# Layer 1's sums regrouped between the steps and a closing part ordered by single operations

## The chip, the cores and the metric

The kernel runs on one core of a Trainium2 chip. A core has five engines with instruction queues of their own: TensorE (PE, matrix products into the accumulators called PSUM), VectorE (DVE), ScalarE (ACT), GpSimd (POOL) and SyncE (SP, which here only issues transfers). [...] The metric is the device time of one launch in microseconds (us), the median of several runs.

## The reference

Two graph layers follow each other over N = 4096 nodes with D = 64 features and one 4096 x 4096 adjacency matrix of zeros and ones.

```python
# layer 0: the last 100 neighbours of a row, weighted by powers of 1/2
rank = cumsum(adj != 0, axis=1); deg = rank[:, -1:]; k = minimum(deg, 100)
w = mask * where(rank - (deg - k) > 0, 0.5 ** (k - (rank - (deg - k))), 0)
x1 = layernorm(x + w @ (x @ W0) + b0)
# layer 1: the mean over the neighbours and the row itself, a dense layer, L2 normalisation
h = (adj @ x1 + x1) / (deg + 1)
z = relu(concat([x1, h]) @ W1 + b1)
out = layernorm(x1 + z / maximum(norm(z), 1e-12))
```

## The kernel before

**Tiles.** The transposed adjacency is cut into 8 slabs `g` of 512 output rows and 8 columns `k` of 512 inputs. A tile `A[g][k]` (128 partitions x 4 x 512, bf16, 512 KB in SBUF) is loaded once by a transfer that POOL issues (`load_next`, line 98), and used twice: for layer 0's weights when it comes in, and for layer 1's sum when all x1 of column `k` is there. The pool `a16` has 33 such buffers; a load waits until one is free.

**The 64 steps** (lines 539 to 576) run over the slabs 0 to 7, each with its columns from 7 to 0. A step has four parts on PE: `weigh` (line 270, 32 small products into two PSUM tiles `v`), some counting (`count`, `spread`), one block of layer 1 (`some_sums`, line 339: four products of 128x512 that add column `k` into slab `g`), and `gather` (line 300, four products of 128x512) for the weights of the step before. The weights `w` are made from `v` by ACT (line 294, the first half) and DVE (line 295, the second half); the next `weigh` writes into the same two PSUM tiles and so waits for both.

**Which blocks** go with the steps is in `jobs` (lines 317 to 321), one list entry for a run of columns of one slab. A run sums in one PSUM bank; at its end `evict_part` (line 331) moves the bank into SBUF: the first time for a slab by a copy on ACT (line 337), later by an addition to `part[g]` on DVE (line 334). The DVE instruction stands in the queue behind the step's `w` and ahead of what is hooked to the step (`run(i, DVE)`). A block may run from step `8(k+1)+7` on. There is one block a step, except in the steps of `SAVED`. Before the change 39 of 64 blocks run with the steps; 25 are left.

**Hooks of layer 0.** For slab `g`, with i = 8(g+1): the projection `first_pz` in step i+1, its moments in i+2, the root (lines 364 to 368) in i+3, x1 itself (line 441, four instructions on DVE) in i+4, its high half (line 446, ACT) and low half in i+5 and i+6, transposes and the dense part c1 until i+8.

**The closing part** (line 759 on) is an order written out by hand: what an engine gets in which order is the order of these calls. It holds layer 0's end for slab 7, the 17 blocks left of slabs 0 to 6 (`own`), slab 7 in two halves of 256 rows (`own_half`, 2 x 8 blocks) and then, for a unit of one or two slabs, a chain: the sum's copy or addition into `hT` (line 627 on DVE, or ACT for slab 7, line 632), `last_pz` (line 659, PE), z (664, DVE), relu and square (668, 673, ACT), the row sums ss (680, 681, DVE), the root (378, POOL, by a power), y (698, DVE), the addition of x1 (703; POOL for a unit of a slab or more, DVE for a half slab), mean and variance (387, 389, DVE), a root on POOL, the output o (748, ACT) and the store (SP). Slabs 3 and 7 share a last root on ACT and DVE, and DVE makes half of their outputs (750). PSUM's eight banks are handed round by the list `banks`; two of its tiles, `va` and `vb`, hold two banks each (lines 582 and 583).

Of the kernel before, what the change touches and what calls it, by code (L numbers as in the profile page):

```python
# [40 lines left out]
def adj_resnorm_kernel(  # L41
# [279 lines left out]
    jobs += [(6, [4, 3, 2, 1, 0, 5]), (4, [4, 5]), (0, [4, 5]), (1, [4, 5]), (2, [4])]  # L321
# [303 lines left out]
    def last_hT(g):  # L625
        ep["hT", g] = hT_of(g)
        nc.vector.tensor_tensor(ep["hT", g], acc[g], part[g], ALU.add)  # L627
        banks.append(acc[g])
# [7 lines left out]
    def unit(*slabs):  # L636
        name, bs = "_".join(map(str, slabs)), [g * TB + t for g in slabs for t in range(TB)]
        n = len(bs)
        tiles = []
        for i in range(n // TB):  # L640
            tiles.append(a16p.tile([P, 4 * TB // n, n, D], F32, tag="a16", name=f"u_{name}_{i}"))
        four = [t[:, i] for t in tiles for i in range(4 * TB // n)]
        return name, bs, four

    def half_unit(h):
        _, bs, four = u7
        ts_ = slice(2 * h, 2 * h + 2)
        return f"{L}{'ab'[h]}", bs[ts_], [f[:, ts_] for f in four]

    def rows(bs):  # L650
        return slice(bs[0], bs[-1] + 1)

    def last_pz(u):

        name, bs, _ = u
        pz = ep["pz1", name] = psum(len(bs), D, f"pz1_{name}")
        for t, b in enumerate(bs):
            h = ep["hT", b // TB]
            nc.tensor.matmul(pz[:, t, :], lhsT=h[:, ts(b % TB, P)], rhs=wn_sb, start=True, stop=True)  # L659

    def last_z(u):

        name, bs, (z, _, _, _) = u
        nc.vector.tensor_tensor(z, ep["pz1", name], c1[:, rows(bs), :], ALU.add)  # L664
        free(f"pz1_{name}")

    def last_relu(u):
        nc.scalar.activation(u[2][1], u[2][0], AF.Relu)  # L668

    def last_sq(u):  # L670
        name, bs, (z, sq, _, _) = u
        if len(bs) >= TB:
            nc.scalar.activation(sq, sq, AF.Square)
        else:
            nc.vector.scalar_tensor_tensor(sq, z, 0.0, z, ALU.max, ALU.mult)

    def last_ss(u):
        name, bs, (_, sq, _, _) = u
        ss = ep["ss", name] = small.tile([P, len(bs)], F32, tag="ss", name=f"ss_{name}")
        nc.vector.tensor_reduce(ss, sq, AX.X, ALU.add)  # L680
        nc.vector.tensor_tensor(ss, ss, least[:, rows(bs)], ALU.max)  # L681

    def last_sn(u):
        name = u[0]
        ep["sn", name] = root_a(ep["ss", name], zero, f"n_{name}")

    def last_rn(u):
        name = u[0]
        ss = ep["ss", name]
        if ("sn", name) in ep:  # L690
            ep["rn", name] = root_b(ep["sn", name], ss, zero, f"n_{name}")
        else:
            ep["rn", name] = root_p(ss, None, name, "rn")

    def last_y(u):
        name, bs, (z, _, y, _) = u
        rn = ep["rn", name].unsqueeze(2).to_broadcast([P, len(bs), D])
        nc.vector.scalar_tensor_tensor(y, z, 0.0, rn, ALU.max, ALU.mult)

    def last_add(u):  # L700
        name, bs, (_, _, y, _) = u
        engine = nc.gpsimd if len(bs) >= TB else nc.vector
        engine.tensor_tensor(y, y, x1[:, rows(bs), :], ALU.add)

    mv_37 = small.tile([P, 2 * TB, 2], F32, tag="mv_37", name="mv_37")
    slot_of = {3: 0, L: TB}

    def last_mv(u):
        name, bs, (_, _, y, _) = u
        if bs[0] // TB in slot_of:  # L710
            ep["mv1", "37"] = mv_37
            t = slot_of[bs[0] // TB] + bs[0] % TB
            moments(y, f"l1_{name}", mv_37[:, t : t + len(bs), :])
        else:
            ep["mv1", name] = moments(y, f"l1_{name}")

    def last_s(u):
        name = u[0]
        ep["s1", name] = root_a(ep["mv1", name][:, :, 1], eps_ln, f"l1_{name}")

    def last_r(u):
        name = u[0]
        v = ep["mv1", name][:, :, 1]
        if ("s1", name) in ep:
            ep["r1", name] = root_b(ep["s1", name], v, eps_ln, f"l1_{name}")
        else:
            ep["r1", name] = root_p(v, LN_EPS, name, "r1")

    def offset(u):
        name, bs, _ = u  # L730
        mv, r = ep["mv1", name], ep["r1", name]
        off = ep["off", name] = small.tile([P, len(bs)], F32, tag="off", name=f"off_{name}")
        if ("s1", name) in ep:
            nc.vector.scalar_tensor_tensor(off, mv[:, :, 0], -1.0, r, ALU.mult, ALU.mult)
        else:
            nc.gpsimd.tensor_tensor(off, mv[:, :, 0], r, ALU.mult)
            nc.gpsimd.tensor_scalar(off, off, -1.0, None, ALU.mult)

    def last_o(u, t0, t1, engine=nc.scalar):
        name, bs, (_, _, y, o) = u  # L740
        if bs[0] // TB in slot_of:
            n0 = slot_of[bs[0] // TB]
            mv, r, off = [ep[what, "37"][:, n0 : n0 + TB] for what in ("mv1", "r1", "off")]
        else:
            mv, r, off = ep["mv1", name], ep["r1", name], ep["off", name]
        for t in range(t0, t1):
            if engine is nc.scalar:
                engine.activation(o[:, t, :], y[:, t, :], AF.Identity, bias=off[:, t : t + 1], scale=r[:, t : t + 1])
            else:
                engine.tensor_scalar(  # L750
                    o[:, t, :], y[:, t, :], mv[:, t, 0:1], r[:, t : t + 1], ALU.subtract, ALU.mult
                )

    def store(u):
        name, bs, (_, _, _, o) = u
        for i, b in enumerate(range(0, len(bs), TB)):
            nc.sync.dma_start(out=out[bs[b] // TB], in_=o[:, b : b + TB, :])

    run(NS, DVE)
    gather(*held)  # L760
    own(5, 5)
    first_hT(L)
    banks.append(ps_a.tile([P, R], F32, tag="acc0", name="va0"))
    first_pz(L)
    own(5, 6)
    first_y(L)
    first_mv(L)
    own(4, 6)
    free(f"pz0_{L}")
    first_s(L)  # L770
    own(0, 6)
    first_least(L)
    first_r(L)
    own(1, 6)
    first_x1(L)
    own(2, 5)
    first_hi(L)
    own_half(1, 0)
    first_xl(L)
    own(6, 6)  # L780
    first_lo(L)
    own(6, 7)
    own(4, 7)
    last_hT(6)
    u6 = unit(6)
    last_pz(u6)
    last_hT(4)
    own(5, 7)
    last_z(u6)
    last_relu(u6)  # L790
    own(1, 7)
    last_hT(5)
    last_sq(u6)
    last_ss(u6)
    own(0, 7)
    last_hT(1)
    last_rn(u6)
    u45 = unit(4, 5)
    last_pz(u45)
    last_hT(0)  # L800
    last_y(u6)
    last_add(u6)
    u01 = unit(0, 1)
    last_pz(u01)
    last_z(u45)
    last_mv(u6)
    last_relu(u45)
    last_sq(u45)
    last_r(u6)
    own(2, 7)  # L810
    last_z(u01)
    last_ss(u45)
    own(2, 6)
    last_relu(u01)
    offset(u6)
    last_sq(u01)
    first_px(L)
    last_rn(u45)
    own(3, 7)
    last_hT(2)  # L820
    first_x1T(L)
    free(f"px_{L}")
    last_ss(u01)
    u2 = unit(2)
    last_pz(u2)
    last_o(u6, 2, 4)
    last_o(u6, 0, 2)
    last_y(u45)
    last_rn(u01)
    first_pu(L)  # L830
    last_z(u2)
    store(u6)
    own(3, 6)
    last_relu(u2)
    first_c1(L)
    free(f"pu_{L}")
    last_sq(u2)
    last_add(u45)
    own_half(1, 6)
    last_y(u01)  # L840
    own_half(1, 7)
    last_ss(u2)
    own(3, 5)
    last_add(u01)
    last_mv(u45)
    own_half(1, 1)
    own_half(1, 4)
    last_rn(u2)
    own_half(1, 3)
    own_half(1, 2)  # L850
    last_hT(3)
    own_half(1, 5)
    last_r(u45)
    last_y(u2)
    u3 = unit(3)
    last_pz(u3)
    last_mv(u01)
    half_hT(1)
    u7 = unit(L)
    u7b = half_unit(1)  # L860
    last_pz(u7b)
    own_half(0, 1)
    last_add(u2)
    last_z(u3)
    own_half(0, 7)
    last_z(u7b)
    last_relu(u3)
    own_half(0, 6)
    last_sq(u7b)
    offset(u45)  # L870
    last_ss(u7b)
    own_half(0, 2)
    last_sq(u3)
    last_r(u01)
    own_half(0, 0)
    last_o(u45, 4, 6)
    last_ss(u3)
    own_half(0, 3)
    last_mv(u2)
    last_sn(u7b)  # L880
    own_half(0, 5)
    last_o(u45, 6, 8)
    own_half(0, 4)
    last_rn(u7b)
    last_o(u45, 2, 4)
    last_rn(u3)
    last_y(u7b)
    half_hT(0)
    last_add(u7b)
    last_o(u45, 0, 2)  # L890
    u7a = half_unit(0)
# [74 lines left out]
```

## Time and profile before

| what | value |
|---|---|
| median of 3 runs | 239.58 us (239.44 to 240.66) |
| the profiled execution's own time | 239.75 us |
| its span, first to last instruction | 238.0 us |
| mean granted PE clock | 0.971 of full speed |
| PE busy | 211.8 us, 89% |
| DVE busy | 180.1 us, 76% |
| ACT busy | 136.2 us, 57% |
| POOL busy | 83.3 us, 35% |
| adjacency transfers | 64, 512 KB each in SBUF |

Busy times are of the whole span. The chain of work that ended last is followed back from the last instruction to what released it. A start-to-start distance of two neighbouring instructions of one engine is what an instruction costs in a full queue; its duration in the trace is a little longer[...].

### The profile page before, as it was taken

The page shows a single profiled execution, that of the slowest core. Times are in us where ns is not written, and L with a number is a line of the kernel's source. Part 1 is how long each engine was busy: PE and PEld are TensorE (multiplying, and loading weights), DVE is VectorE, ACT ScalarE, POOL GpSimd, SP SyncE. Part 2 cuts the span into 40 slices and gives each one's busy share as a digit, 9 for nine tenths or more (in the row PEclk, how much of TensorE's full clock was granted, in tenths as well). Part 3 has the DMA queues.
Part 4 walks back from the last instruction along what each step waited for, and adds up shares of the span by engine and source line. Part 5 has one row for each costly group of instructions (what it writes and reads, how often), then busy time and mean ns, then how long its engine had stood idle before and what let it go on. Part 6 is the DMA issues. An engine that isn't in the chain of part 4 may idle for free.

```text
span 238.0 us, 7425 instructions
## 1 busy us (share of the span) xinstructions
PE 211.8 (89%) x3128; PEld 98.4 (41%) x3171; DVE 180.1 (76%) x457; ACT 136.2 (57%) x205; POOL 83.3 (35%) x160
## 2 busy tenths in 40 slices
PE   8689979889997999999999999999999999996920
PEld 2223324234433533443345344434453354765810
DVE  5459788987896699778847975686768765789973
ACT  6058876788676756653655456555645521171582
POOL 8344573432432311213221152214610000277940
PEclk9799999999999999999999999999999999999795
DMA  6999999999999999999999999999930000000021
GB/s 200 209 216 220 212 213 212 222 215 213 220 213 215 214 222 213 212 213 218 218 208 186 193 206 185 187 178 183 196 77 3 3 0 0 3 1 23 3 88 66
DMA packets 11985, 37.34 MB, mean 157 GB/s; under 512 B 1328, under 2 KB 3504, under 8 KB 11952
## 3 DMA queue, kind: packets, MB, share of 16 engines
q0 software_dynamic: 9216, 33.56, 72.4%
q1 hardware_dynamic: 2736, 3.31, 4.5%
q8 instruction: 25, 0.41, 0.6%
q14 instruction: 8, 0.07, 0.1%
HBM read 69.37 MB, written 1.05 MB: 296 GB/s over the span
## 4 chain that ended last, share of the span: by engine, by line
PE 47%; DMA 34%; issue 7%; DVE 7%; POOL 2%; ACT 2%; ACTq 0%; POOLq 0%
DMA a<-in_adjT_dram 34%; PE acc L305 11%; PE acc_part L314 10%; PE v L278 5%; PE cnt L248 4%; PE v L287 3%; PE va L659 2%; PE va L314 2%; PE vb L608 2%; PE pi L528 2%; PE rep L266 1%; PE vb L314 1%; PE ma L314 1%; PE pz L414 1%; ACT w L294 1%
## 5 line engine op out<-in xcount | busy, mean ns | idle before, releaser
L294 ACT ACTIVATE w<-v,less 128x1024 int16<-128x1024 f32 x64 | 71.3, 1113 | 50.4 <-PE v L287 38.0
L295 DVE TENSOR_SCALAR w<-v 128x1024 int16<-128x1024 f32 x64 | 78.2, 1222 | 19.1 <-PE v L287 17.7
L105 POOL DMA_DIRECT2D a<-in_adjT_dram x64 | 35.8, 560 | 97.0 <-PE rep L266 34.4
L305 PE MATMUL acc<-w,xhl 128*128 128x512 bf16 x240 | 66.1, 379 | 2.1 <-issue 1.1
L314 PE MATMUL acc_part<-a,x1hl 128*128 128x512 bf16 x132 | 37.3, 381 | 2.1 <-issue 1.4
L305 PEld LDWEIGHTS <-xhl 128*128 128x128 f16 x256 | 23.1, 98 | 32.7 <-issue 9.1
L268 ACT ACTIVATE near<-rep,most 128x512 bf16<-128x512 f32 x39 | 26.6, 682 | 8.2 <-PE rep L266 8.1
L314 PEld LDWEIGHTS <-x1hl 128*128 128x128 f16 x224 | 18.6, 98 | 30.4 <-issue 14.4
L278 PE MATMUL v<-a,tri 32*32 32x512 bf16 x1024 | 28.7, 385 | 0.5 <-ACT w L294 0.5
L287 PE MATMUL v<-near,mine 32*32 32x512 bf16 x1024 | 27.7, 376 | 0.0
L248 PE MATMUL cnt<-a,pick 128*32 128x512 bf16 x256 | 21.2, 386 | 6.5 <-DMA a<-in_adjT_dram 4.9
L258 DVE TENSOR_TENSOR cs<-cnt,cs 128x512 bf16<-128x512 f32 x31 | 21.2, 685 | 6.4 <-PE cnt L248 6.3
L278 PEld LDWEIGHTS <-tri 32*32 32x32 bf16 x1024 | 9.7, 88 | 19.7 <-issue 19.3
L378 POOL TENSOR_TENSOR rn<-ss,power 128x4 f32<-128x4 f32 (+1 forms) x5 | 6.3, 1276 | 29.0 <-DVE ss L681 28.9
L266 PE MATMUL rep<-cs,further 128*128 128x512 bf16 x39 | 15.0, 385 | 1.0 <-DVE cs L258 1.0
L248 PEld LDWEIGHTS <-pick 128*32 128x32 bf16 x256 | 6.0, 94 | 21.5 <-issue 12.6
L233 POOL TENSOR_TENSOR a<-a,ident_b 128x128 bf16<-128x128 bf16 x32 | 12.7, 429 | 0.1
L287 PEld LDWEIGHTS <-mine 32*32 32x32 bf16 x1024 | 10.3, 87 | 2.5 <-issue 2.4
L659 PE MATMUL va<-wts,hT 128*128 128x64 f32 x64 | 8.8, 292 | 2.4 <-DVE hT L627 1.9
L260 DVE CAST cs<-cnt 128x512 bf16<-128x512 f32 x8 | 5.5, 691 | 6.7 <-PE cnt L248 6.7
L659 PEld LDWEIGHTS va<-wts,hT 128*128 128x128 f32 x64 | 8.4, 206 | 3.7 <-DVE hT L627 2.8
L668 ACT ACTIVATE u<-u 128x256 f32<-128x256 f32 (+1 forms) x5 | 2.5, 502 | 12.4 <-DVE u L664 12.4
(136 smaller groups left out, 241.5 us busy)
## 6 DMA issues: line engine op xcount, KB each, us to landing
a<-in_adjT_dram POOLq DMA_DIRECT2D x64, 512.0 KB, 16.5
c<-in_x_quads_dram SPq DMA_DIRECT2D x2, 512.0 KB, 4.5
x<-in_x_dram SPq DMA_DIRECT2D x8, 128.0 KB, 7.3
out_dram<-u SPq DMA_DIRECT2D x8, 128.0 KB, 1.7
wts<-in_weights_dram SPq DMA_DIRECT2D x1, 160.0 KB, 7.2
```

Of the source, the lines that this page charges most:

```text
L105: nc.gpsimd.dma_start(out=a, in_=adjT[g, k])
L248: nc.tensor.matmul(cnt[g][quarters[q], :], lhsT=pick[:, PW - 4 * k : PW - 4 * k + Q], rhs=A[g][k][:, q, :], start=first, stop=last,)
L258: nc.vector.tensor_tensor(new, cnt[g], cs[g], ALU.add)
L266: nc.tensor.matmul(pr, lhsT=further, rhs=cs[g], start=True, stop=True)
L268: nc.scalar.activation(near[g], pr, AF.Relu, bias=most, scale=-1.0)
L278: nc.tensor.matmul(v[e // 2][quarters[q], e % 2, :], lhsT=tri[quarters[e], :], rhs=A[g][k][quarters[e], q, :], start=True, stop=False,)
L287: nc.tensor.matmul(v[e // 2][quarters[q], e % 2, :], lhsT=mine[quarters[e], 4 * k + q, :], rhs=nr[quarters[e], :], start=False, stop=True,)
L294: nc.scalar.activation(w[:, 0:2, :], v[0], AF.Relu, bias=less)
L295: nc.vector.tensor_scalar(w[:, 2:4, :], v[1], -STEP * MAX_NEIGH, 0.0, ALU.add, ALU.max)
L305: nc.tensor.matmul(acc0[g], lhsT=xhl[:, b, :], rhs=w[:, q, :].bitcast(BF16), start=(k, q) == (NK - 1, 0), stop=(k, q) == (0, KB - 1),)
L314: nc.tensor.matmul(acc, lhsT=x1hl[:, b, :], rhs=A[g][b // KB][:, b % KB, :], start=first, stop=last)
L659: nc.tensor.matmul(pz[:, t, :], lhsT=h[:, ts(b % TB, P)], rhs=wn_sb, start=True, stop=True)
```

## The change

First, `jobs` gets another fifth line. Slab 6 is left wholly to the closing part, as are columns 6 and 7 of every slab; 36 blocks run with the steps and 28 are left. In steps 51 to 60 other blocks run than before, most of them a run of their own; steps 61 to 63 get none.

Second, the closing part is written anew. Every operation has a name in `work`, and one string gives the order of all of them, so that the instructions of one phase (the eight of a mean and variance, the four of a root) can stand apart with others between them. Small results lie in one tile `scratch`. The arithmetic of a unit is as it was, with these differences: x1 is added on DVE for every unit (`DVE_ADDS`), the sum of slab 6 is copied to `hT` by ACT (`COPIED`, it has no `part`), the offset on POOL is the negated mean times the root, and in the last group DVE makes five outputs and ACT three (before four and four).

```diff
-    jobs += [(6, [4, 3, 2, 1, 0, 5]), (4, [4, 5]), (0, [4, 5]), (1, [4, 5]), (2, [4])]
+    jobs += [(0, [4]), (1, [4]), (2, [4]), (4, [4, 5]), (5, [5]), (3, [5]), (0, [5]), (1, [5]), (2, [5])]
...
-    def last_hT(g):
+    def slab_hT(g):
         ep["hT", g] = hT_of(g)
-        nc.vector.tensor_tensor(ep["hT", g], acc[g], part[g], ALU.add)
+        if g in COPIED:
+            nc.scalar.copy(ep["hT", g], acc[g])
+        else:
+            nc.vector.tensor_tensor(ep["hT", g], acc[g], part[g], ALU.add)
         banks.append(acc[g])
...
+    UNITS = ['6', '45', '01', '2', '3', '7b', '7a']
+    COPIED = (6,)
+    DVE_ADDS = ('6', '45', '01', '2', '3', '7b', '7a')
+    SHARED = ('3', '7b', '7a')
...
-        engine = nc.gpsimd if len(bs) >= TB else nc.vector
-        engine.tensor_tensor(y, y, x1[:, rows(bs), :], ALU.add)
+        adder = nc.vector if u in DVE_ADDS else nc.gpsimd
+        work["add" + u] = lambda: adder.tensor_tensor(y, y, x1[:, rows, :], ALU.add)
...
+            for t in range(n):
+                full, tt = (str(L), t + 2 * halves[u]) if u in halves else (u, t)
+                by_dve = tt >= (1 if u in halves else 2)
...
+    order = """
+        gather own6_0 fhT fpz ownha_5 y0 own1_6 bn_L0_3 ag_L0_3 bn_L0_0 bn_L0_2 bn_L0_1 own5_6 ag_L0_2 ag_L0_1
+        ag_L0_0 deg s0 least least2 qa_r0 own4_6 qb_r0 qc_r0 qd_r0 x1_1 own2_6 x1_2 x1_3 x1_0 hi own0_6 xl lo
+        ownha_1 own4_7 own1_7 hT4 own0_7 hT1 px hT0 own5_7 x1T pz01 hT5 pz45 z01 relu01 sq01 pu z45 own2_7 ss01
+        relu45 own6_7 ssm01 sq45 t1 rn01 hT2 own6_6 c1 pz2 ss45 y01 own6_1 ssm45 z2 rn45 add01 own6_2 relu2 sq2
+        bn_01_4 bn_01_7 own3_6 ag_01_4 bn_01_0 bn_01_3 ss2 bn_01_5 own6_4 ag_01_3 y45 bn_01_1 own6_3 ssm2 add45
+        rn2 bn_45_5 own6_5 bn_45_4 bn_45_0 ag_45_5 bn_45_3 bn_45_2 bn_45_1 bn_45_6 own3_7 ag_45_1 hT6 ag_45_6
+        ag_45_2 ag_45_3 ag_45_4 bn_45_7 ag_45_0 ag_01_1 ag_45_7 pz6 bn_01_6 neg45 ag_01_5 ag_01_7 ag_01_6 eps45
+        hT3 pow45 ownha_4 z6 pz3 ag_01_0 bn_01_2 relu6 ag_01_2 y2 sq6 ownhb_7 add2 neg01 ownha_3 ss6 of45 o45_2
+        ownha_7 eps01 ssm6 bn_2_0 rn6 ag_2_0 o45_6 bn_2_2 ownha_6 bn_2_3 bn_2_1 o45_1 ownhb_4 ag_2_1 z3 o45_4
+        ownha_0 y6 pow01 relu3 ownha_2 add6 sq3 ownhb_5 o45_7 bn_6_1 bn_6_0 ss3 hT7a ownhb_1 o45_5 ag_6_1 ag_6_0
+        pz7a bn_6_2 of01 ssm3 ag_6_2 st45_4 bn_6_3 o01_5 rn3 ownhb_3 ag_6_3 z7a o01_3 ag_2_2 ownhb_0 sq7a o01_0
+        ss7a ownhb_2 o01_4 neg6 y3 o01_7 ownhb_6 eps6 ssm7a ag_2_3 add3 pow6 sn7a hT7b qa_n7a bn_3_3 qb_n7a
+        o01_6 bn_3_2 pz7b ag_3_3 bn_3_1 o01_1 st01_4 bn_3_0 of6 qc_n7a z7b o6_1 neg2 ag_3_2 sq7b eps2 o6_3
+        qd_n7a pow2 ss7b o6_0 ag_3_1 ssm7b ag_3_0 y7a sn7b o6_2 qa_n7b add7a o01_2 qb_n7b of2 st6_0 bn_7a_1
+        qc_n7b o2_1 bn_7a_0 st01_0 qd_n7b ag_7a_0 o2_0 y7b ag_7a_1 o2_3 add7b bn_7b_0 o2_2 bn_7b_1 ag_7b_0
+        ag_7b_1 st2_0 sS o45_0 qa_S qb_S o45_3 qc_S qd_S st45_0 offS o7_3 o7_0 o7_2 o7_1 o3_0 o3_2 st7 o3_1 o3_3
+        st3
+    """
     run(NS, DVE)
-    gather(*held)
-    own(5, 5)
-    first_hT(L)
...
-    store(u3)
+    for name in order.split():
+        work.pop(name)()
```

In the string, `own6_0` is block `own(6, 0)`; `ownha_k` and `ownhb_k` are blocks of slab 7's first and second half; `fhT` to `c1` are layer 0's end; and for a unit such as 01 (slabs 0 and 1), `pz`, `z`, `relu`, `sq`, `ss`, `ssm` (the maximum), `rn` (the root), `y`, `add`, `bn` and `ag` (moments of a block of 128 rows), `neg`, `eps`, `pow`, `of` (POOL), `o` and `st` are the chain's links. `qa` to `qd` are a root's four instructions on DVE, `sn` and `sS` a root on ACT.

## The prediction

> **What bounds the kernel now.** I read the page's busy times and 40 slices first, then the chain of work that ended last, then the instructions in order of time where it changes hands.
>
> ```profile
> PE 211.8 (89%) x3128; PEld 98.4 (41%) x3171; DVE 180.1 (76%) x457; ACT 136.2 (57%) x205; POOL 83.3 (35%) x160
> PE   8689979889997999999999999999999999996920
> PEclk9799999999999999999999999999999999999795
> DMA  6999999999999999999999999999930000000021
> ```
>
> PE is full until slice 36; the transfers end near 178 us. So the early part goes with the DMA (34% of the chain) and the later steps and the closing part with PE. At the end the chain reads (start, length, engine and result):
>
> ```profile
> 218.92 0.54 DVE mv_l L389 x8
> 219.47 0.58 DVE hT L627
> 220.09 2.32 PE va L659 x12
> 222.42 4.38 PE vb L608 x32
> 226.82 0.38 ACT hT L632
> 227.25 0.67 PE va L659 x4
> 227.94 0.30 DVE u L664
> ```
>
> PE stands still before 220.09 (1.94 us, for slab 3's `hT`, which is queued on DVE behind moments), and again 0.46 us before 227.25. From 227.94 on a chain of small DVE and ACT instructions needs 10.06 us to the end. In short stretches (PE, PE loads, DVE, ACT, POOL busy, clock, DMA):
>
> ```profile
> 220.00:220.50 0.50, 0.41 (x4) 0.41 (x4) 0.50 (x4) 0.00 (x0) 0.50 (x1) 1.00 0.00 0
> 221.00:221.50 0.50, 0.50 (x4) 0.50 (x4) 0.50 (x7) 0.00 (x0) 0.50 (x1) 0.50 0.00 0
> 224.00:224.50 0.50, 0.50 (x6) 0.42 (x5) 0.50 (x5) 0.50 (x2) 0.50 (x1) 0.92 0.00 0
> ```
>
> After the gap the clock is halved from about 220.7 to 224.05: 3.4 us of work at half rate, 1.7 us lost. Two more readings, DVE in order of time at steps 51 to 53, and DVE beside POOL in the closing part:
>
> ```profile
> 156.95 1.23 DVE L295 TENSOR_SCALAR w<-v 128x1024 int16<-128x1024 f32 x1 [0.40 <-PE v L287]
> ...
> 159.16 1.22 DVE L295 TENSOR_SCALAR w<-v 128x1024 int16<-128x1024 f32 x1 [0.25 <-PE v L287]
> 160.30 1.41 DVE L441 TENSOR_SCALAR x<-y,mv_l,r_l 128x64 f32<-128x64 f32 x4
> 161.64 1.21 DVE L295 TENSOR_SCALAR w<-v 128x1024 int16<-128x1024 f32 x1
> ...
> 214.71 1.76 DVE L698 SCALAR_TENSOR_TENSOR u<-u,rn 128x512 f32<-128x512 f32 x1
> ```
>
> DVE has 0.25 us to spare before step 52's `w` and none before step 53's. ACT's cast (161.81) and then its `w` (162.12 to 163.23) wait for that x1, and step 54's `weigh` (163.28) starts 0.05 us after it.
>
> **What the Trainium skill says.** "TensorE: Matmul & The Clock Gate", Part 1: activity is judged in free-running windows of 3413 ns, and an idle one leaves the array at half rate. The trace agrees in length (3.4 us at 0.50), but the window before, 217.25 to 220.66, was still 43% busy. "GPSIMD Engine Reference", Specifications: POOL shares its SBUF access with DVE and contends with instructions of two SBUF inputs; the trace agrees, 1.76 us for the y at 214.71 beside POOL's addition (214.51 to 215.92), 0.69 alone. "PSUM — Partial Sum Buffer", Summary: another bank may be read while PE writes, guarded by bank; the program guards more coarsely (below). "VectorE: DVE Perf Modes", The DRAIN you can't avoid: a semaphore between two instructions costs nothing extra. The trace differs: 0.71 us from a 512-wide sum to an instruction that needs it, 0.61 between independent ones.
>
> **Steps 51 to 60.** Same number of blocks, same tiles released in the same steps, so PE and loads keep their work. But nine runs end there with an addition on DVE (steps 51, 52, 53, 55 to 60) instead of two (58 and 60; one more, in 56, ended with an ACT copy): seven additions of 0.60 us (183.78 to 184.38) in new places. I walk DVE: `w` of step 51 156.95, its eviction 158.10 to 158.70, root (0.81) to 159.51, so `w` of 52 is 0.35 late and ends 160.65; eviction to 161.25; then x1. It cost 1.34 us in all beside POOL's four diagonal additions (160.84 to 162.42) and 0.89 without (184.38 to 185.27). Now it lies inside POOL's stretch: three at 0.39, one at 0.23, to 162.65, 1.0 later than before. Cast, `w` on ACT and step 54's `weigh` follow: 164.2 instead of 163.28, **0.93 us lost** (bounds 0.5 without contention, 1.15). The additions of steps 53, 55 and 57 go into idle time of 0.88, 1.66 and 1.62 us on DVE, and those of 56 and 59 end before PE needs the `w` behind them; without that cover each costs 0.6. Step 57 is nearest: the count's sum is done about 0.1 us before `spread` needs it.
>
> **Steps 61 to 63** lose three blocks of 0.864 us (195.72 to 196.58). Step 61's was free: at 186.91 PE was waiting 0.17 us for ACT. In step 62 PE would be free at 188.70, ACT's and DVE's `w` end 188.83 and 188.9, so `weigh` starts at 188.97 instead of 189.56: 0.6. In step 63 the last `gather` waits for ACT's `w` (0.8 + 1.11 after `weigh`): another 0.6. **1.2 us won** of 2.6; the closing part starts 0.27 us earlier.
>
> **PE in the closing part** gets 3 x 0.864 = **2.6 us** more. Against it stand the waits. Before: 2.1 (with the last product's drain), 0.45 and the 1.7 of the slow clock, 4.25 together. After, from a `gather` end at 191.73 if the steps cost nothing (all times below are then 0.9 later): layer 0's end takes 5.1 us from `fpz` to `lo` as before and is covered by five blocks and two halves (5.2). Slab 0's `hT` ends at 202.55, `pz01` and `pz45` (0.23 us a block of 128 rows) at 204.4 and 206.25. Both write the tile `vb`, one bank each, and the built program lets `z01` wait for PE's count at the end of `pz45`: 1.84 us later than its data. Then `z01` 206.28, relu and square on ACT 207.01 to 208.30, ss 208.36, its maximum 209.07, `t1` 209.15, and only then `hT2`, 209.49 to 210.18. PE has done `pu`, `own2_7`, `own6_7`, `own6_6` by 209.06 and stands before `pz2`: **1.15 us**. DVE goes on without idling through two units; `hT3` ends at 218.3, and `ownha_4`, in the same PSUM tile, waits 0.2 for it. Slab 7's second half costs its copy's 0.45 as before; 0.15 lies before `pz01`. 1.95 in all, no slow window assumed: **2.3 won**.
>
> DVE itself: the additions cost 3 x 0.34 + 2 x 0.61 = 2.2 us more, one output 0.24; `hT6` on ACT saves 0.61, the two stalls beside POOL 1.15 and 0.97. It comes out level, and PE still sets the pace. ACT's 0.6 for `hT6` fits ahead of `pz6`, covered by `own3_7`.
>
> **The sum to the last z:** -0.27 + 2.6 - 2.3 = 0.0, thus 228.0.
>
> **The tail.** From the last z to the last root on ACT it was 4.25 us (227.94 to 232.19), eight of the moments of slab 2 and eight of the half slab's among it. The new order puts y, addition and moments of 7a into the waits of 7b's root; link by link (0.33 from a half's operation to one that needs it, 0.23 else) it gives 3.7. Then 2.86 to the last output becomes 2.5, since ACT makes three of 0.355 instead of four. The store's 2.95 stay. **0.9 won.**
>
> Span 238.0 - 0.85 = 237.15; own time 1.75 more, 238.9. The runs' median lay 0.17 below the profiled execution: **238.7 us**, 0.4% faster, which counts as no change: about 0.5%, or 1.2 us, is what a measurement of this kernel can tell.
>
> **Rivals.**
> *The clock drops again.* The 1.15 us gap before `pz2` halves the rate for one window: 1.7 us less 0.1 absorbed by later waits, **240.3**, slower than before. For it: 57% idle of a window was enough. Against: 26% (12.45 to 15.87, with a gap of 0.7) was not, and 1.15 is 34%. It decides from wherever between these the limit lies.
> *DVE becomes the bound in steps 51 to 60*: none of the seven evictions is covered, 4.2 us instead of 0.93, **242.0**. It decides once DVE's work in a step, 3.2 us in steps 51 and 59 against some 2.7 to 3.4 of PE's, exceeds PE's over several steps. Against: DVE idles in between (1.66 us before step 56's `w`).
> *Both delays are hidden*: x1 is not late and `hT2` comes in time, 2.0 less, **236.7**. For it: only one queue position makes each. Against: both follow from orders within a queue.
> That an eviction or a block is simply dropped is excluded: the built program has all 64.
>
> **How the numbers follow.** The forecast 0.47, both hidden 0.22, the clock 0.20, DVE 0.11. My steps add some 20 durations each good to 0.05 and two waits good to 0.3: about 1 us either way, so the forecast's own range is 237.6 to 239.8. The whole range, 237.0 to 240.6, leaves out DVE's case and about half of "both hidden". Faster than 238.4: a third of the forecast and nearly all of "both hidden", 0.37. Slower than 240.8: a third of the clock's case and most of DVE's, 0.16. The rest, 0.47.
>
> **What would show it.** Step 54's `weigh` near 164.2; the closing part's first block near 192.7; a PE gap of about 1.1 us before slab 2's projection near 211 and none of 0.5 besides the last; a clock of 1.00 up to the last projection; no DVE instruction of 1.7 us; last z near 228, last ACT root 3.7 us after it. The prediction is wrong if the wait of `z01` for `pz45` isn't there, if a slow window follows the gap, or if DVE falls behind over several steps.

## The result, and the profile after

The changed kernel takes 240.57 us in the median of 15 runs (239.52 to 241.72), the kernel before 239.34 beside it (238.34 to 240.66): a ratio of 1.0049, 95% interval 1.0027 to 1.0071. In a second comparison it was 240.12 against 239.62, 1.0018 (1.0003 to 1.0033). It is a little slower, by 0.03% to 0.7%; the forecast was 238.7, a little faster. The profiled execution took 241.19 us with a span of 238.1.

The page of the kernel after (busy times, slices, clock, transfers):

```profile
PE 209.1 (88%) x3128; PEld 96.9 (41%) x3171; DVE 183.3 (77%) x467; ACT 136.0 (57%) x204; POOL 78.5 (33%) x155
PE   8587789989978999999999999998999799989930
PEclk9999999999999999999999999999999999999995
DMA  6999999999999999999999999999940000000023
```

PE's busy times (211.8 us before, 209.1 after) can't be compared: each page has 3128 of the 3171 products, not the same ones, and a second profile of the changed kernel, which has all 3171, gives 215.4. The clock is not halved before the last product (mean 0.989); in the profile before (0.971) it is halved twice, from 9.04 to 12.45, which left step 51 no later (its `w` is at 156.95, and at 157.15 in a second profile without that window), and from 220.67 to 224.08. DVE has 3.2 us more, POOL 4.8 less. The chain of work that ended last, in the closing part (start, length, engine and result):

```profile
204.29 3.80 PE vb L757 x32
...
208.11 0.70 DVE u L760
...
211.37 0.61 DVE hT L710
...
212.03 1.10 PE va L757 x8
213.13 1.73 PE ma L314 x8
...
221.71 3.93 PE va L608 x36
...
227.82 0.38 ACT hT L715
...
228.25 0.67 PE va L757 x4
...
228.94 0.29 DVE u L760
```

Both projections of slabs 0, 1, 4 and 5 come first (204.29, 32 products), then `z01`, a chain through ACT and DVE to slab 2's `hT`, and slab 2's projection at 212.03. DVE starts its instructions in the order of the string (`ssm01` at 210.87, `t1` 210.96, `hT2` 211.29, `c1` 211.89, `ss45` 212.22), so `hT2` comes after all that stands ahead of it. From 212.03 PE carries the chain to the last z. PE's one large gap (PE in order of time), and the busy times in the window of 3.41 us in which it lies. The windows are counted back from the drop of the clock after the last product, at 233.12 (columns: PE, PE loads, DVE, ACT, POOL busy, clock, transfers):

```profile
212.03 1.10 PE L757 MATMUL va<-wts,hT 128*128 128x64 f32 x8 [1.13 <-DVE hT L710]
```
```profile
209.23:212.64 3.41, 2.28 (x14) 1.20 (x12) 2.62 (x7) 2.01 (x4) 1.46 (x1) 1.00 0.01 2
```

PE is busy in two thirds of that window, and the clock stays at 1.00. Steps 51 to 54, DVE in order of time and then PE's `weigh` of step 54:

```profile
157.27 1.22 DVE L295 TENSOR_SCALAR w<-v 128x1024 int16<-128x1024 f32 x1 [0.40 <-PE v L287]
158.41 0.68 DVE L334 TENSOR_TENSOR part<-acc_part,part 128x512 f32<-128x512 f32 x1
...
159.74 1.22 DVE L295 TENSOR_SCALAR w<-v 128x1024 int16<-128x1024 f32 x1
160.88 0.68 DVE L334 TENSOR_TENSOR part<-acc_part,part 128x512 f32<-128x512 f32 x1
161.47 1.53 DVE L441 TENSOR_SCALAR x<-y,mv_l,r_l 128x64 f32<-128x64 f32 x4
162.93 1.21 DVE L295 TENSOR_SCALAR w<-v 128x1024 int16<-128x1024 f32 x1
```
```profile
164.56 0.44 PE L278 MATMUL v<-a,tri 32*32 32x512 bf16 x16 [0.98 <-ACT w L294]
```

The two evictions stand ahead of x1, which takes 1.53 us for its four, and `weigh` waits 0.98 us for ACT's `w`.

To compare traces whose starts differ by up to 0.8 us, I use distances: from step 51's `w` (DVE) to the first closing block, from that block to `z01` and to the last z, and from the last z to the end of the span.

| trace | `w` to first block | block to `z01` | block to last z | last z to end | span |
|---|---|---|---|---|---|
| before, first profile | 36.02 | | 34.97 | 10.0 | 238.0 |
| before, second profile | 36.01 | | 33.35 | 10.5 | 237.0 |
| after, first profile | 35.79 | 15.05 | 35.88 | 9.2 | 238.1 |
| after, second profile | 35.80 | 15.06 | 35.90 | 9.2 | 237.7 |
| another tile for 45 | 35.79 | 12.96 | 33.85 | 9.2 | 236.2 |
| that, and x1 later | 34.93 | 12.97 | 33.90 | 9.2 | 234.6 |

The steps win 0.22 us, and the tail (last z to end) 0.8 to 1.3. The closing part up to the last z loses 0.9 against the first profile of before, and 2.5 against the second: that is where the result comes from.

### The profile page after: what moved, and what is told of

The parts are those of the page before. It is cut to its first block, busy times and chain, and to the rows that moved or that the text cites. A ratio compares the mean times of both kernels' runs of the same rounds, so it can differ in the third digit from the quotient of the medians.

```text
span 238.1 us, 7425 instructions
## 1 busy us (share of the span) xinstructions
PE 209.1 (88%) x3128; PEld 96.9 (41%) x3171; DVE 183.3 (77%) x467; ACT 136.0 (57%) x204; POOL 78.5 (33%) x155
## 4 chain that ended last, share of the span: by engine, by line
PE 51%; DVE 10%; ACT 4%; issue 2%; ACTq 0%; DVEq 0%
PE acc L305 12%; PE acc_part L314 11%; PE v L278 6%; PE cnt L248 4%; PE v L287 3%; PE va L608 3%; PE vb L757 2%; ACT w L294 2%; PE ma L314 2%; DVE w L295 2%; PE pz L414 2%; PE va L314 1%; PE rep L266 1%; DVE part L334 1%; DVE x L441 1%
## 5 line engine op out<-in xcount | busy, mean ns | idle before, releaser
L314 PE MATMUL acc_part<-a,x1hl 128*128 128x512 bf16 x123 | 34.5, 382 | 1.9 <-issue 1.3
L774 POOL TENSOR_TENSOR scratch<-scratch,power 128x4 f32<-128x4 f32 (+1 forms) x5 | 6.7, 1349 | 35.1 <-DVE scratch L776 34.9
L334 DVE TENSOR_TENSOR part<-acc_part,part 128x512 f32<-128x512 f32 x18 | 12.2, 679 | 0.0
L446 ACT CAST x1hl<-x 128x256 f16<-128x256 f32 x8 | 3.2, 405 | 12.5 <-DVE x L441 10.5
L788 ACT ACTIVATE u<-u,scratch 128x64 f32<-128x64 f32 x27 | 9.7, 428 | 1.1 <-POOL scratch L807 0.6
```

What stands on the lines that cost most here:

```text
L314: nc.tensor.matmul(acc, lhsT=x1hl[:, b, :], rhs=A[g][b // KB][:, b % KB, :], start=first, stop=last)
L334: nc.vector.tensor_tensor(part[g], acc, part[g], ALU.add)
```

## The experiments

Times are medians. The kernel before was run beside each group: 239.63, 239.62, 239.74 and 239.24 us in the four.

| run | median us | ratio to before, 95% interval | median span |
|---|---|---|---|
| before again | 239.78 | 1.0014 (0.9990 to 1.0039) | 237.9 |
| list of runs alone | 243.94 | 1.0192 (1.0144 to 1.0240) | 242.1 |
| closing part alone | 242.24 | 1.0123 (1.0077 to 1.0168) | 240.2 |
| another tile for 45 | 238.05 | 0.9932 (0.9911 to 0.9953) | 235.9 |
| after again | 240.12 | 1.0018 (1.0003 to 1.0033) | 237.9 |
| three blocks less | 241.60 | 1.0088 (1.0056 to 1.0119) | 239.5 |
| four additions less | 239.88 | 1.0026 (1.0006 to 1.0047) | 237.9 |
| four additions on POOL | 244.13 | 1.0198 (1.0167 to 1.0230) | 242.1 |
| another tile, x1 later | 237.20 | 0.9903 (0.9871 to 0.9936) | 235.0 |
| old list, earlier hT | 241.17 | 1.0067 (1.0044 to 1.0089) | 238.7 |
| before, hT3 earlier | 239.51 | 1.0006 (0.9985 to 1.0026) | 237.5 |
| z01 sooner | 237.75 | 0.9932 (0.9905 to 0.9958) | 235.8 |

### The kernel before again

No edit.

> The kernel before, unchanged, for the span and the granted clock of each of its runs and for a second trace. Theory A (the walk was right in its waits, the miss is elsewhere): the half-rate window after the gap before slab 3's projection is there again, most runs show a clock near 0.971 as the first profile did, and spans near 238.0. Theory B (that window belonged to the one profiled execution, so 1.7 us were counted as won that the usual run never lost): most runs have a clock of 0.978 or more and spans of 236.3 to 237.2; the second trace has a clock of 1.00 from 220 us to the last projection.

Both theories are half right. In the 65 runs of before in this group the span is 237.9 in the median, as in the first profile. But they fall into groups: the 20 runs with a clock of 0.984 or more have spans of 236.6 to 237.3, the 18 with 0.971 to 0.973, like the first profile, 237.6 to 239.2 and nearly all near 237.9. The other 27 have clocks between these or lower and spans of 236.9 to 240.9, and no profile here is one of theirs. The mean clock doesn't say where a half-rate window lies (six of the fourteen profiles have one that starts between 8.3 and 9.1 us), nor how soon the clock drops after the last product. A clock of 0.984 or more leaves no room for either. The second profile is one of that group. It has the same gap before slab 3's projection, and no half rate after it (PE in order of time):

```profile
220.29 1.55 PE L659 MATMUL va<-wts,hT 128*128 128x64 f32 x12 [1.94 <-DVE hT L627]
```

The clock's windows tell why. Busy times in those around the gap, counted as above: the first profile, then the second:

```profile
217.26:220.67 3.41, 1.47 (x14) 1.14 (x12) 3.41 (x22) 0.37 (x1) 2.67 (x4) 1.00 0.00 0
220.67:224.08 3.41, 3.41 (x18) 2.90 (x18) 3.06 (x22) 1.77 (x6) 3.16 (x6) 0.50 0.00 0
```
```profile
216.39:219.80 3.41, 1.96 (x18) 1.50 (x16) 3.38 (x20) 0.37 (x1) 2.34 (x3) 1.00 0.00 0
219.80:223.21 3.41, 2.92 (x27) 2.77 (x28) 3.34 (x22) 0.71 (x2) 3.16 (x6) 1.00 0.00 0
```

In the first the whole gap lies in one window, which is 43% busy, and the next runs at half rate. In the second the grid cuts the gap in two, and the windows are 57% and 86% busy: the rate stays. The grid stands differently in each execution. What a halved window costs shows between the two traces: from step 51's `w`, the last z comes 1.6 us later and the end 1.16 us later. What bounds the undisturbed execution stands in its chain of work that ended last:

```profile
214.91 1.76 DVE u L698
216.67 0.34 DVE ss L680
...
219.12 0.54 DVE mv_l L389 x8
219.66 0.57 DVE hT L627
220.23 0.33 DVE u L698
...
226.16 0.42 DVE u L698
226.58 0.23 DVE u L664
```

Every piece from 214.91 to the last z is DVE, which is busy 11.25 of these 11.6 us. PE's wait of 1.94 us before 220.29 and the 0.49 before 225.82 lie beside it, off the chain. POOL is close behind: its root for slab 3 ends at 226.13, and DVE's y, the piece at 226.16, needs it. Where the clock is halved PE gets onto the chain, as in the profile that the prediction was read from.

### Slab 3's hT earlier in the kernel before

```diff
     last_add(u01)
+    last_hT(3)
     last_mv(u45)
...
-    last_hT(3)
     own_half(1, 5)
```

> The kernel before with one line moved: slab 3's hT is added ahead of the moments of slabs 4 and 5 on VectorE, 1.6 us earlier in its queue. The wait of 1.94 us before slab 3's projection should shrink to under 0.6 and the half-rate window after it go, in each theory. TensorE sets the pace, so that its waits are won when they go (the prediction's sum): 1.5 of wait and the lost half of a window where there was one, so 237 us or less in the median and spans of 235.3 in its undisturbed runs. VectorE is as full as TensorE there, so that the wait only moves behind its backlog: undisturbed runs keep spans of 236.5 to 237.2, and only the runs that had the half-rate window gain about 1.1: median 238.6 to 239.2.

The wait goes from 1.94 to 0.39 us, and comes back in another place (PE in order of time):

```profile
218.38 1.55 PE L659 MATMUL va<-wts,hT 128*128 128x64 f32 x12 [0.39 <-DVE hT L627]
...
225.93 0.66 PE L659 MATMUL va<-wts,hT 128*128 128x64 f32 x4 [2.50 <-ACT hT L632]
```

2.50 us of wait for slab 7's `hT`, where there were 0.49: first block to last z is 33.93, not less than 33.35. The lowest spans are 237.2, not 235.3. So a wait of PE in the closing part of the kernel before was worth nothing when it went. DVE's queue is not the whole reason. The chain that ended last goes through POOL here, from 219.98 to 226.36:

```profile
219.98 0.34 POOL r L376
220.40 1.67 POOL r L378
...
223.72 1.67 POOL r L378
225.38 0.98 POOL rn L378
...
226.39 0.42 DVE u L698
```

These are the roots of slabs 4 and 5, of 0 and 1, and of slab 3. They start when the moments of slabs 4 and 5, which `hT3` has passed on DVE, are done: 0.6 us later than in the second profile of before, counted from step 51's `w`, and the last z is later by the same 0.6. DVE waits 0.31 us for the last of them, and ACT's copy of slab 7's `hT`, whose products end at 223.43, starts at 225.53, behind outputs that had waited for POOL's offset: that is PE's 2.50 us. DVE and POOL are both nearly full (5.88 and 6.09 of the 6.5 us from 219.9).

The median (239.51) is not below 239.24 either, and 15 of the 22 runs show a clock of 0.970 to 0.974. In the profiled one the grid cuts the new gap and the rate stays; that the gap, longer than the old one, halves the rate in others fits their clocks, but no trace shows it, and their spans (from 237.2) start where those at 0.981 and 0.982 do.

### Slabs 4 and 5's projection in another tile

```diff
-    banks += [ma, one_acc, va[:, 0, :], vb[:, 0, :], va[:, 1, :], vb[:, 1, :], mb]
+    banks += [ma, one_acc, va[:, 0, :], mb, va[:, 1, :], vb[:, 1, :], vb[:, 0, :]]
```

> The changed kernel, in which slabs 4 and 5's projection goes to another PSUM tile than slabs 0 and 1's, so that the addition z01 waits for slabs 0 and 1's projection alone. If the shared tile makes the wait before slab 2's projection: z01 starts about 1.8 us sooner after its own projection's end, the wait of 1.13 us is gone or under 0.2, and the time is about 1.0 below the changed kernel's, near 239.5. If VectorE's queue makes the wait (z01 finds it busy anyway) or the time only moves to a later wait: less than 0.4 below, near 240.4.

238.05, 2.0 below the changed kernel: twice what was expected. DVE in the closing part, first the changed kernel, then this one:

```profile
202.35 1.29 DVE L710 TENSOR_TENSOR hT<-vb,part 128x512 f32<-128x512 f32 x2 [2.44 <-PE vb L314]
203.55 1.44 DVE L710 TENSOR_TENSOR hT<-va,part 128x512 f32<-128x512 f32 x2
208.11 1.29 DVE L760 TENSOR_TENSOR u<-vb,c 128x512 f32<-128x512 f32 x2 [3.12 <-PE vb L757]
```
```profile
201.56 0.69 DVE L710 TENSOR_TENSOR hT<-vb,part 128x512 f32<-128x512 f32 x1 [1.58 <-PE vb L314]
...
206.11 0.69 DVE L760 TENSOR_TENSOR u<-vb,c 128x512 f32<-128x512 f32 x1 [1.04 <-PE vb L757]
207.89 0.69 DVE L760 TENSOR_TENSOR u<-mb,c 128x512 f32<-128x512 f32 x1 [1.09 <-PE mb L757]
```

The shared tile makes two waits, not one. `z01` waited for slabs 4 and 5's projection, as predicted; and slab 4's `hT` at 202.35 waited until slab 1's block, in the other bank of `vb`, was through as well, so that slab 0's `hT` came 0.2 us late for `pz01`. With both gone `z01` starts 2.09 us sooner after the first block, PE has no wait before slab 2's projection (210.52), and the last z comes 2.03 us sooner. The gain is `z01`'s whole delay, not PE's gap of 1.13.

### After again, and which engine is full

> The changed kernel, unchanged, beside the kernel before on one chip, for its ratio, its spans and a second trace. If the loss is real and lies in the closing part: spans near 238.0 in nearly all runs, 1.1 us above those runs of before that show a clock of 0.984 or more (236.6 to 237.3), and a stretch from the first closing block to the last z of 35.9 us again. If the first comparison was chance: a ratio under 1.001. The time outside the span: 2.0 or more in the median, against 1.79 of before, if it belongs to the kernel; 1.8 if it was chance.

Real, and in the closing part: 35.90 us from the first block to the last z, as in the first profile. The time outside the span is 1.96 us in the median against 1.81 for before, so this too belongs to the kernel. Now two kernels that leave work out:

```diff
+    left[6] = [k for k in left[6] if k not in (2, 3, 4)]
...
-        ... own6_2 ... own6_4 ... own6_3 ...
```

> The changed kernel with three of slab 6's blocks left out (its columns 2, 3 and 4, 2.6 us of TensorE between slab 2's and slab 6's projections; slab 6's result lacks them). TensorE sets the pace of the closing part, as the prediction has it: 2.2 to 2.6 faster, near 238.0. VectorE sets it from z01 on, where it idles only 1.4 us up to the last z: at most 0.7 faster, 239.8 or more, with TensorE's waits before the later projections grown by some 2 us.

```diff
-        ... add01 ... add45 ... add2 ... add6 ...
```

> The changed kernel without four of the additions of x1 that VectorE makes (units of slabs 0 and 1, 4 and 5, 2, 6: 2.2 us of VectorE; their rows lack x1). TensorE sets the pace: under 0.3 faster, near 240.4. VectorE alone sets it: 2.0 or more faster, near 238.4. Both are full from z01 on, so that neither's relief helps for long: 0.3 to 0.8 faster, and three blocks less gives about as little.

From `z01` to the last z the changed kernel takes 20.83 us. Without 2.6 us of PE's work it takes 20.50, without 2.2 us of DVE's 20.84 (the median, 239.88, is 0.24 below the changed kernel's, the figure for "TensorE sets the pace"; the first result excludes that PE alone does). So neither engine alone sets the pace: take work from one, and the other is in the way. With three blocks less PE runs ahead and waits for DVE (PE in order of time; then busy times in the two windows of the clock's grid around the wait):

```profile
219.88 0.60 PE L609 MATMUL va<-a,x1hl 128*128 128x256 bf16 x4 [2.44 <-DVE hT L711]
```
```profile
215.29:218.70 3.41, 2.16 (x14) 1.38 (x13) 3.38 (x22) 0.59 (x1) 1.39 (x1) 1.00 0.01 2
218.70:222.11 3.41, 2.23 (x21) 2.09 (x21) 3.27 (x19) 1.06 (x3) 2.78 (x6) 1.00 0.00 0
```

DVE is busy throughout. Worse, the median is 1.5 us above the changed kernel's, though the profiled run's span is 237.8: here the grid cuts the gap (63% and 65% busy), and the clock is 0.989; the five other runs have 0.969 to 0.976 and spans of 239.0 to 240.4. That those are halved windows after the gap fits the clocks, though no trace of theirs is there. In the profiled run, then, the three blocks cost 0.33 of their 2.6 us, since DVE needs nearly all of that time anyway; that they also keep the rate up is likely, but not shown.

### The additions of x1 on GpSimd

```diff
-    DVE_ADDS = ('6', '45', '01', '2', '3', '7b', '7a')
+    DVE_ADDS = ('3', '7b', '7a')
```

> The changed kernel with these four additions on GpSimd again, as before the change; nothing is left out. By the prediction the move is level for VectorE, since its instructions beside GpSimd's additions stretch (1.76 for 0.69): within 0.4 of the changed kernel, and two VectorE instructions of 1.5 us or more in the closing part. If the additions are worth more off VectorE than the stretching costs: 0.5 to 1.5 faster. If GpSimd's own 1.4 us for each delays the moments behind them: 0.5 to 1.5 slower, with new waits of VectorE on GpSimd's u.

4.0 us slower than the changed kernel, far beyond the last case. DVE waits for POOL's results, and no instruction of DVE in the closing part is stretched to 1.5 us (the profile is of the slowest of the five runs, 246.73 us):

```profile
217.78 0.35 DVE L649 BATCH_NORM_STATS2 scratch<-u 128x6 f32<-128x64 f32 x2 [2.65 <-POOL u L781]
221.01 0.48 DVE L649 BATCH_NORM_STATS2 scratch<-u 128x6 f32<-128x64 f32 x3 [1.24 <-POOL u L781]
...
230.08 0.35 DVE L649 BATCH_NORM_STATS2 scratch<-u 128x6 f32<-128x64 f32 x2 [1.87 <-POOL u L781]
```

In the new order the moments stand shortly behind the addition; with POOL between, slab 3's `hT` behind them comes late (PE waits 2.54 us for it), and two half-rate windows follow, from 223.66 to 230.49. What of the 4.0 us is wait and what is clock was not separated. In this order, at any rate, the additions belong on DVE.

### Each half of the change alone

The list of runs, with the old closing part. The order has slab 6's six more blocks instead of the three that now run with the steps (so three more than before, not nine as the expectation below says), and ACT copies slab 6's sum:

```diff
-    own(5, 5)
+    own(6, 0)
...
-    own(2, 5)
+    own(6, 1)
...
-    own(6, 6)
+    for k in (2, 3, 4, 5, 6):
+        own(6, k)
...
-    own(3, 5)
```

> The kernel before with the new list of runs alone, and the old closing part, which only makes the nine missing blocks in the places of those that are done now and copies slab 6's hT on ScalarE. By the prediction's terms: 0.93 lost at x1, 1.2 won in steps 61 to 63, 2.6 more of TensorE work in the closing part, and the old waits of 2.1 and 0.45 stay: 2.3 slower than before, near 241.7 (if the half-rate window stays as it was). Rival (the steps are where the change loses, beyond x1): 3 us or more slower, with DVE or ScalarE ending the waits of steps 55 to 60. Rival (the new blocks fill the old waits): within 1 us of before. Step 54's product should start near 164.2 to 164.6 in each.

243.94, 4.3 above before: the loss of the second case, but not its place. The steps are as in the changed kernel, 35.80 us from `w` to the first block. In the closing part, with the blocks in the places that I gave them, PE waits 2.99 us for slab 3's `hT` on DVE (1.94 before), and the clock is halved after it.

The new closing part with the old list of runs (own5_5 in the place of own6_0, own2_5 ahead of own2_7, own3_5 for own6_1, own6_2 to own6_5 left out, slab 6's `hT` added on DVE):

> The changed kernel with the old list of runs, so that the closing part has nine sums fewer to copy and three blocks less: the new order of single operations alone. By the prediction's terms: no late x1, no 2.6 of TensorE work, waits 2.3 and tail 0.9 won: 3.2 faster than before, near 236.2. Theory B (1.7 of the waits won were never lost in the usual run): 1.5 faster, near 237.8. Rival (the new order is worse in itself, its wait before slab 2's projection costs as much as the old ones): 239 or more.

242.24, against every figure but the last. PE waits 2.90 us for slab 6's `hT`, which DVE makes here and which stands behind the moments of slabs 4 and 5. So I moved it, and slab 3's, forward:

```diff
-  ... c1 pz2 ss45 ... own3_7 ag_45_1 hT6 ag_45_6 ... eps45 hT3 pow45 ...
+  ... c1 pz2 hT6 ss45 ... own3_7 hT3 ag_45_1 ag_45_6 ... eps45 pow45 ...
```

> The new closing part with the old list of runs once more, but slab 6's and slab 3's hT in earlier places of VectorE's queue. If the 2.9 us wait of the first trial and the half-rate window behind it came from slab 6's place in that queue: no wait over 1 us, a clock of 0.978 or more in most runs, and about 236.0 to 236.6 of span, near 238.3, since slabs 0 and 1's projection has a tile of its own there. If the three blocks fewer are what is missing (TensorE runs ahead of VectorE wherever hT stands): waits of 2 us or more in all before later projections, a half-rate window in most runs, and 240.5 or more.

The wait is 2.58 us now, for slab 3's `hT`, and 241.17 us is what the second theory gave:

```profile
219.06 1.84 PE L757 MATMUL va<-wts,hT 128*128 128x64 f32 x8 [2.58 <-DVE hT L710]
```

That projection alone takes 1.84 us instead of 1.10, at half rate. `z01` starts 12.97 us after the first block here, and still the last z is 36.45 after it. In the orders tried, the two parts of the change need each other: without the new list's blocks PE runs ahead in the new order and waits for DVE, and in the old order they only add time.

### Slab 5's x1 one step later

On top of the other tile:

```diff
+        d = 1 if g == 5 else 0
-        at(i + 4, DVE, first_x1, g)
-        at(i + 5, ACT, first_hi, g)
+        at(i + 4 + d, DVE, first_x1, g)
+        at(i + 5 + d, ACT, first_hi, g)
```

and likewise for `xl`, `lo`, `px`, `x1T`, `pu` and `c1`.

> The kernel with slabs 4 and 5's projection in another PSUM tile, in which slab 5's x1 and the six steps that follow from it are each made one step later, behind step 53's w instead of ahead of it. If the two new evictions ahead of x1 hold up step 54's product, as the prediction has it: from step 51's w on VectorE to step 54's product 6.3 us as in the kernel before, instead of 7.3; the closing part's first block 0.9 sooner after that w; and the time about 0.9 below that kernel's 238.05, near 237.2. If the delay only moves (the later x1 holds up steps 55 to 57, or the gain is lost at the next wait for VectorE): the first block where it was, within 0.3 of 238.05.

237.20, as expected. DVE in steps 51 to 54, and PE's `weigh` of step 54:

```profile
156.58 1.23 DVE L295 TENSOR_SCALAR w<-v 128x1024 int16<-128x1024 f32 x1 [0.40 <-PE v L287]
...
161.20 1.22 DVE L295 TENSOR_SCALAR w<-v 128x1024 int16<-128x1024 f32 x1 [0.34 <-PE v L287]
...
162.94 0.97 DVE L441 TENSOR_SCALAR x<-y,mv_l,r_l 128x64 f32<-128x64 f32 x4
```
```profile
162.83 0.43 PE L278 MATMUL v<-a,tri 32*32 32x512 bf16 x16
```

6.25 us from step 51's `w` to step 54's `weigh`, where the changed kernel has 7.29; x1, no longer beside POOL's additions (160.47 to 162.04), takes 0.97. The first closing block comes 0.86 us sooner. This kernel is 1.0% faster than before and 1.2% faster than the changed one.

### z01 sooner still

```diff
-  ownha_1 own4_7 own1_7 hT4 own0_7 hT1 px hT0 own5_7 x1T pz01 hT5 pz45 z01 relu01 sq01 pu z45 own2_7 ss01
+  ownha_1 own1_7 own0_7 hT1 own4_7 hT0 px hT4 pz01 own5_7 x1T z01 relu01 sq01 hT5 own2_7 pu pz45 ss01 z45
```

> The best kernel so far (another tile for slabs 4 and 5's projection, slab 5's x1 a step later) in which slabs 1, 0 and 4 get their column 7 first, slabs 0 and 1's projection follows at once, and slab 5's block and projection come behind it. From z01 on both engines are full, so what counts is when z01 starts: it comes some 0.8 us sooner after the first closing block (12.1 instead of 12.97), and the time falls by 0.4 to 0.8, to 236.4 to 236.8. If TensorE's amount of work alone counts: no change, 237.2. If slabs 4 and 5's later z gives it back: 237.2 or more, with a VectorE wait for it of 1 us or more.

`z01` comes 12.16 us after the first block, as meant, but the median is 237.75, half a microsecond worse. The intervals of the two ratios overlap; the traces show the loss, 34.72 us from the first block to the last z instead of 33.90. `z45` starts at 207.60 after a DVE wait of 1.04 us, 15.93 after the first block instead of 14.76. So here it counted when DVE had both units, not the first alone.

## Why the prediction was wrong

**Right: the steps.** `weigh` of step 54 was to start 0.93 us late; it is 0.96 (7.29 from `w` instead of 6.33). The closing part was to start 0.27 sooner; it is 0.22. Moving x1 gave the 0.9 back, so the cause is as told.

**Right: what stands where.** The gap before slab 2's projection (1.15 foreseen, 1.13), the wait of `z01` for slabs 4 and 5 through the shared tile, no half rate before the last product, no stretched DVE instruction, 20.8 us from `z01` to the last z (20.83), 3.7 from there to the last root (3.68), 2.5 to the last output (2.53).

**Wrong: the sum of waits, and that "PE still sets the pace".** This is the step that failed: 2.6 us of new PE work were set against 2.3 us of PE's waits won. From the first block to the last z the changed kernel takes 0.9 us more than the first profile of before, so 1.7 were won, and 2.5 more than the second, so 0.1 were won. What was won against the first is about the halved window (1.6 us to the last z); the waits themselves were hardly there to be won. In the second profile they lie beside a chain that is DVE from 214.91 to the last z, and taking 1.5 us of one away won nothing, since POOL's roots then came 0.6 later. In the changed kernel PE does carry the chain from 212.03 on, but with 2.6 us less to do it was only 0.33 sooner. Of the 1.7 us for the halved clock, 1.16 reach the end, and only in executions that have it. Against the runs of before without it (spans near 236.9) the new span is 1.0 to 1.1 us longer. That the medians lie only 0.2% to 0.5% apart fits this: the old gap halves the rate in many runs of before, and the new one, by the windows seen here, doesn't (1.13 us leave 67% of a window, if PE is busy in the rest).

**Wrong: the size of one term, 0.5 us.** `z01` was to start 14.55 us after the last `gather`; it is 15.05. Layer 0's end was taken as 5.1 us "as before" and covered by 5.2 us of blocks. From `fpz`'s last product (194.94) to the end of `lo` (200.36) it takes 5.4 (5.2 before, counted the same way), since in the new order the root is asked 1.58 us after y (1.38 before), so PE waits 0.28 before slab 4's last block; and slab 0's `hT` came 0.2 late for `pz01`, also by the shared tile.

**Wrong: what lies outside the span.** 1.75 us and 0.17 less for the median were taken over from before; the changed kernel has 2.0 in the median, and 3.1 in the profiled execution. There, one packet of instructions lands after the span's end (transfers from 239 to 242 us, after a span of 238.1):

```profile
q8 instruction: 1, 0.02, 2.0%
```

Of the fourteen profiles here four have such a packet, and they are the four with the most time outside the span: 3.1, 2.8, 3.3 and 2.2 us, against 1.8 to 2.1 in the ten without. That the long ones wait for these instructions fits, but was not tested, nor what decides whether the packet comes that late; and the 0.2 of the median stays open. More than 2.2 us lie outside the span in 25 of 147 runs of before, too, and in 9 of 37 of the changed kernel.

With a span of 237.15, 0.5 for `z01` and 2.0 outside, the forecast would have been 239.65. The median span (237.9 and 238.0 in the two groups) lies 0.25 and more above the 237.65 in that sum, and the two medians of the time were 240.12 and 240.57; that rest is not explained.

**The rivals.** "Both delays are hidden" was to end 2.0 us lower. Both delays were there, and taking both away by other means gave 237.2, 2.9 below the changed kernel: the delays were real, and the tile was priced at half its worth (1.15 for 2.0), because the price was read from PE's gap while DVE's whole queue moved. The clock's rival did not come true: the window 67% busy kept its rate. DVE as the bound of steps 51 to 60 did not come true either; DVE was at the bound in the closing part, where the prediction had called it level.

## What to carry to other kernels

Before a wait is counted as won, ask whether the other engines would be ready any sooner: here PE's waits lay in the shadow of a DVE that was busy 97% of the time, with POOL's roots close behind, and a second profile of the same kernel showed the chain there. Take a wait's price from how far it moves the queue that is full, not from the gap that it leaves on one engine, and read more than one profile: two executions of one kernel had different engines on the chain. Work that fills such a shadow costs little. Two banks in one tile were one wait for this program.

## What was not expected of the hardware

The clock went by the windows of a grid of its own, not by gaps: every half-rate stretch before the last product is 3.41 or 6.83 us long. Of the full-rate windows in the closing parts of all fourteen traces, those up to 47% busy were followed by half rate, those of 57% or more were not; of two between, one 51% busy kept the rate and one 53% busy lost it, a difference of 0.07 us, which the modelled ends of the products may make. The Trainium skill, "TensorE: Matmul & The Clock Gate", Part 1, has the free-running windows but speaks of idle ones; here about half a window of idling was enough. The same gap of 1.94 us was thus followed by a half-rate window, and an end 1.16 us later, in one execution and not in the next; the place of the grid is the difference that the two traces show. And in four of fourteen profiles a packet of the program's own instructions landed after its last instruction.
